# Weight differences of a feed-forward block: GpSimd subtractions replaced by accumulating DMAs, their signs kept in DRAM

## The chip, the core and the metric

The kernel runs on one core of one Trainium2 chip. The metric is the time of one execution in device microseconds; the time before is the median of three runs, 2515.53 us (2514.8 to 2521.83). A core has TensorE (PE, matrix products; PEld is its weight load), VectorE (DVE), ScalarE (ACT), GpSimd (POOL) and SyncE (SP, which here does nothing but issue DMAs), each with a queue of its own that it works through in order, and 16 DMA engines that serve the DMAs of every queue.

## The reference, cut to what matters

Two sequences of 512 tokens, 1024 features, pass three residual blocks: a scan layer with its own gated MLP, a cross product with a quantized context, and a feed-forward block whose weights are made from pairs of matrices:

```python
def _binary_diff_weight(w, base):
    d = w - base
    coeff = jnp.mean(jnp.abs(d))
    return base + coeff * jnp.sign(d)
W1 = _binary_diff_weight(w1, mean_w1)      # each 3584 x 1024 (W2: 1024 x 3584)
W2 = _binary_diff_weight(w2, mean_w2)
W3 = _binary_diff_weight(w3, mean_w3)
h = silu(x @ W1.T) * (x @ W3.T)
return h @ W2.T
```

The mean of |d| runs over the whole matrix, so no weight can be made before all of its pair has been read once. The MLP of the first block has the same form, with plain weights gate_w, up_w and down_w.

## The kernel before, in words

Everything is computed in float32 on tiles of 128 partitions. The stages, by the span of the profiled execution: norms, input projections and scan up to about 370 us; the scan's output product (L564) and the second norm; then a gate loop for the MLP ("m", about 462 to 1150), a down product (to about 1480), and the same two for the feed-forward block ("f": gate loop from about 1497 to 2240, down product to the end).

Each gate loop (`gates`, L646) has 14 rounds of 256 hidden features. A round takes a gate weight, an up weight and a down weight, each 1 MiB, a tile of 128 x 2048. The products go by a seven-product block scheme: `weight_blocks` (L210) forms sums of weight blocks on VectorE, `BlockProduct` (L227) makes 28 matmuls per product into four PSUM banks, and ScalarE copies the first partial product out (`p1`, L249) so that the next additions can use it. `others` (L254) lets TensorE go on with 12 matmuls before one must wait for an addition that reads `p1`. Silu is at L672, the product of gate and up at L677. `down_blocks` (L274) forms the combinations of the down weight, stored to DRAM at L668; the hidden blocks are stored at L680 to L685. The down product (`down`, L691) loads these combinations back into 12 operand tiles, whose order in memory is the argument `places`, behind an empty region of `space` elements per partition.

The differences are needed twice. During the m loop `side` calls `abs_sums` (L824) in each round: for each of the three pairs it loads raw weight and base (1 MiB each, SP), subtracts them on GpSimd (L827) and sums the absolute values on ScalarE (L828, `accum_out`). `find_coeff` (L857) makes the three coefficients during the m down product. During the f loop `ffn_weight` (L975) loads the pair again, subtracts on GpSimd (L984), takes the sign on ScalarE (L985) and forms base + coeff * sign on VectorE (L986) into the weight tile. The first two weights of the f loop are made before it begins (`begun`, L989), between the m down product, the last context products (L905 to L918, with the queries of L887) and the norm that fills `x3T` (L920).

The order of the instructions on each engine is fixed when the program is built, by a scheduler that places them by its own costs; it is not the order of the source. `side` work therefore runs ahead of the rounds it is called in: in SP's queue the 33rd raw weight of `abs_sums` stands ahead of the load of gate 9. Tiles come from pools (`POOLS`, L627) with a fixed number of buffers, and a load waits until the buffer's last reader is done: two weight buffers `w` for gate and up, two `raw` and two `base` for the pairs, one `t8` for the down weight.

Of the kernel before, what the change touches and what calls it, by code (L numbers as in the profile page):

```python
# [10 lines left out]
F32 = mybir.dt.float32  # L11
BF16 = mybir.dt.bfloat16
AF = mybir.ActivationFunctionType
ALU = mybir.AluOpType
# [3 lines left out]
P = 128  # L18
NB = 2
L = 512  # L20
D = 1024
KC = D // P
# [3 lines left out]
GW = 256  # L26
NG = INTER // GW
# [10 lines left out]
def decoder(ctx, tc, a, out):  # L38
    nc = tc.nc
# [3 lines left out]
    acts = ExitStack()  # L43
# [128 lines left out]
    def flat(tl):  # L172
        return tl.rearrange("p a b -> p (a b)")

    def load_w(wp, tag, src, name, shape=(P, KC, GW)):
        wt = wp.tile(list(shape), F32, tag=tag, name=name)
        nc.sync.dma_start(wt, src)
        return wt

    def tiles_waited(**kw):  # L180
        return tc.tile_pool(reuse_waits="tile", **kw)
# [15 lines left out]
    def act_blocks(name, act, tiles):  # L197

        b11, b21 = act[0][:, :4, :], act[0][:, 4:, :]
        b12, b22 = act[1][:, :4, :], act[1][:, 4:, :]  # L200
        t2, t3, t4 = tiles
        for c in range(TPB):
            cs = slice(c * P, c * P + P)
            sub(t3[:, :, cs], b22[:, :, cs], b12[:, :, cs])
            sub(b12[:, :, cs], b12[:, :, cs], b11[:, :, cs])
            sub(t2[:, :, cs], b22[:, :, cs], b12[:, :, cs])
            sub(t4[:, :, cs], b21[:, :, cs], t2[:, :, cs])
        return {1: b11, 2: b21, 3: b22, 4: t4, 5: b12, 6: t2, 7: t3}

    def weight_blocks(pool, name, w):  # L210

        a11, a12 = w[:, :4, :P], w[:, 4:, :P]
        a21, a22 = w[:, :4, P:], w[:, 4:, P:]
        s = pool.tile([P, 3, 4, P], F32, tag="s", name=f"{name}s")
        s2, s3, s4 = (s[:, i, :, :] for i in range(3))
        sub(s3, a11, a21)
        add(a21, a21, a22)
        sub(s2, a21, a11)
        sub(s4, a12, s2)
        return {1: a11, 2: a12, 3: s4, 4: a22, 5: a21, 6: s2, 7: s3}  # L220
# [53 lines left out]
    def down_blocks(t8):  # L274


        b12, b11, b21, b22, t1, t2, t3, t4 = (t8[:, i, :] for i in range(8))
        sub(t3, b22, b12)
        sub(t1, b12, b11)
        sub(t2, b22, t1)  # L280
        sub(t4, b21, t2)

    def hidden_blocks(h):

        a11, a12, a22, a21, s2, s3, s4 = (h[:, i, :] for i in range(7))
        sub(s3, a11, a21)
        add(a21, a21, a22)
        sub(s2, a21, a11)
        sub(s4, a12, s2)
# [4 lines left out]
    with ExitStack() as m:  # L294
# [9 lines left out]
        sp = proj.enter_context(tiles_waited(name="wsum", bufs=2))  # L304
        pl = {
            "p1": proj.enter_context(tiles_waited(name="wp1", bufs=2)),
            "tmp": proj.enter_context(tiles_waited(name="wtmp", bufs=3)),
        }
# [12 lines left out]
        def load_win(g, i):  # L321
            return load_w(wa, "w", a["w_in"][g, i], f"win{g}_{i}")
# [34 lines left out]
        for i, top in enumerate((0, 4, 5)):  # L357
            w = load_win(0, i)
# [191 lines left out]
        h2T = []  # L550
# [73 lines left out]

    POOLS = dict(t8=1, w=2, raw=2, ap=1, sp=2, hp=1, tmp=7, p1=2)  # L627

    def open_pools(g, name, names):

        pl = {x: g.enter_context(tiles_waited(name=f"{name}{x}", bufs=POOLS[x])) for x in names}
        return pl
# [13 lines left out]
    def gates(name, act, acts, g, pl, weights, side, begun):  # L646


        dram = [
            [tc.dram_tile([P, 7, 512], F32, name=f"{name}{x}d{i}") for i in range(NG)] for x in ("h", "w")  # L650
        ]
        with g:
            B = act_blocks(name, act, [pl["ap"].tile([P, 4, L], F32, tag=f"t{i}", name=f"{name}t{i}") for i in (2, 3, 4)])
            for i in range(NG):
                gw, uw, t8 = weights(i)
                if i == 0:
                    gate, up = begun
                    gate.B = up.B = B
                else:
                    gate, up = (  # L660
                        BlockProduct(
                            (odd, 2 + odd, 4 + odd, 6 + odd), pl, f"{name}{x}{i}",
                            weight_blocks(pl["sp"], f"{name}{x}{i}", w), B,
                        )
                        for odd, (x, w) in enumerate((("g", gw), ("u", uw)))
                    )
                down_blocks(t8)
                nc.sync.dma_start(dram[1][i], t8[:, 1:, :])  # L668
                gc = gate.others() if i == 0 else gate.whole()
                sg = [gate.t("s")] + list(gc[1:])  # L670
                for o, c in zip(sg, gc):
                    nc.scalar.activation(o, c, AF.Silu)  # L672
                side(i, pl["raw"])
                uc = up.others() if i == 0 else up.whole()
                h = pl["hp"].tile([P, 7, L], F32, tag="h", name=f"{name}h{i}")
                for slot, s_, u_ in zip((0, 3, 1, 2), sg, uc):
                    nc.vector.tensor_tensor(h[:, slot, :], s_, u_, ALU.mult)  # L677
                last = i == NG - 1
                if last:
                    nc.sync.dma_start(dram[0][i][:, :3, :], h[:, :3, :])  # L680
                hidden_blocks(h)
                if last:
                    nc.sync.dma_start(dram[0][i][:, 3:, :], h[:, 3:, :])
                else:
                    nc.sync.dma_start(dram[0][i], h)  # L685
        acts.close()
        return dram
# [116 lines left out]
    sums = const.tile([P, 3, NG], F32, name="sums")  # L804
    FFN = (("w1", "mean_w1"), ("w3", "mean_w3"), ("w2", "mean_w2"))

    g = ExitStack()
    pl = open_pools(g, "m", ("t8", "w", "raw", "ap", "sp", "hp", "tmp", "p1"))
    cx = g.enter_context(tiles_waited(name="cx", bufs=1))

    def mlp_weights(i):
        gw = load_w(pl["w"], "w", a["gate_w"][i], f"gate{i}")
        uw = load_w(pl["w"], "w", a["up_w"][i], f"up{i}")
        t8 = pl["t8"].tile([P, 8, 512], F32, tag="t8", name=f"down{i}")
        nc.sync.dma_start(t8[:, :4, :], a["down_w"][i])
        return gw, uw, t8

    def ffn_pair(wp, n, i, why):
        return [
            flat(load_w(wp, tag, a[x][i], f"{why}{x}{i}", (P, 4, 512) if n == "w2" else (P, KC, GW)))  # L820
            for tag, x in (("raw", n), ("base", f"mean_{n}"))
        ]

    def abs_sums(i, wp):  # L824
        for j, (n, _) in enumerate(FFN):
            w, base = ffn_pair(wp, n, i, "s")
            nc.gpsimd.tensor_tensor(w, w, base, ALU.subtract)  # L827
            nc.scalar.activation(w, w, AF.Abs, accum_out=sums[:, j, i : i + 1])  # L828
        if i < KC:
            ctx_codes(i // 4, i % 4)  # L830

    loaded = [mlp_weights(0)]
    begun = first_products("m", h2T, pl, *loaded[0][:2])
    dram = gates("m", h2T, acts, g, pl, lambda i: loaded.pop() if loaded else mlp_weights(i), abs_sums, begun)


    acts = ExitStack()
    x3T = [acts.enter_context(tc.tile_pool(name="x3a", bufs=1, side="right", reuse_waits="tile")).tile([P, KC, L], F32, name="x3T0")]
# [16 lines left out]
    coeff = const.tile([P, 3], F32, name="coeff")  # L855
# [114 lines left out]
    x3T.append(acts.enter_context(tiles_waited(name="x3b", bufs=1)).tile([P, KC, L], F32, name="x3T1"))  # L970

    g = ExitStack()
    pl = open_pools(g, "f", ("p1", "sp", "w", "ap", "hp", "raw"))

    def ffn_weight(i, j):  # L975
        n = FFN[j][0]
        w, base = ffn_pair(pl["raw"], n, i, "f")
        if n == "w2":
            to = pl["t8"].tile([P, 8, 512], F32, tag="t8", name=f"fw2{i}")
            dst = to[:, :4, :].rearrange("p a b -> p (a b)")  # L980
        else:
            to = pl["w"].tile([P, KC, GW], F32, tag="w", name=f"f{n}{i}")
            dst = flat(to)
        nc.gpsimd.tensor_tensor(w, w, base, ALU.subtract)  # L984
        nc.scalar.activation(w, w, AF.Sign)  # L985
        nc.vector.scalar_tensor_tensor(dst, w, coeff[:, j : j + 1], base, ALU.mult, ALU.add)  # L986
        return to

    begun = [ffn_weight(0, 0), ffn_weight(0, 1)]  # L989

    def ffn_weights(i):
# [4 lines left out]
    first = first_products("f", x3T, pl, *begun)  # L996
# [2 lines left out]
    for t in range(TPB, NT):  # L999
        contexts[1].normed(t)  # L1000
    q.close()
    pl.update(open_pools(g, "f", ("t8", "tmp")))

    def store(t0, dh):

        j = t0 < TPB
        for cs in [slice(512 * j + Q * dh, 512 * j + Q * dh + Q)] + [slice(512 * (1 - j) + Q * dh, 512 * (1 - j) + Q * dh + Q)]:
            src = pairs[t0 // 2][:, :, cs]
            nc.sync.dma_start(out[t0 * P : (t0 + 2) * P, cs].rearrange("(a p) n -> p a n", p=P), src)

    dram = gates("f", x3T, acts, g, pl, ffn_weights, lambda i, wp: None, first)
    down("f", dram, 10752, (2, 3, 4, 8, 5, 6, 0, 7, 1, 9, 10, 11), store, lambda: None)


# [50 lines left out]
```

## Time and profile before

| what | value |
|---|---|
| median of three runs | 2515.53 us (2514.8 to 2521.83) |
| profiled execution | 2520.54 us, span 2518.6 us, granted TensorE clock 0.990 |
| TensorE busy | 2446.3 us (97% of the span) |
| VectorE, ScalarE, GpSimd busy | 1462.9, 487.3, 487.9 us |
| DMA | 475.39 MB, mean 189 GB/s |
| GpSimd subtractions L827, L984 | 42 each, 198.8 and 209.5 us busy |
| ScalarE L828, L985 | 42 each, 80.3 and 80.2 us busy |
| VectorE L986 | 42, 98.6 us busy |
| loads of raw weight and base, first loop | 42 and 42 of 1024 KB, 8.9 and 10.5 us from issue to landing |
| the same, second loop | 42 and 42 of 1024 KB, 5.0 and 8.4 us |

The span is from the first to the last instruction; the execution's own time is about 2 us more. The page cuts the span into 40 slices and gives each engine's busy share of a slice in tenths, the granted clock, and the mean share of the 16 DMA engines. A wait is put down to what ended last before it ended. TensorE's busy time says when it had work, not that it ran at its peak.

### The profile page before, as it was taken

The page shows a single profiled execution, that of the slowest core. Times are in us where ns is not written, and L with a number is a line of the kernel's source. Part 1 is how long each engine was busy: PE and PEld are TensorE (multiplying, and loading weights), DVE is VectorE, ACT ScalarE, POOL GpSimd, SP SyncE. Part 2 cuts the span into 40 slices and gives each one's busy share as a digit, 9 for nine tenths or more (in the row PEclk, how much of TensorE's full clock was granted, in tenths as well). Part 3 has the DMA queues.
Part 4 walks back from the last instruction along what each step waited for, and adds up shares of the span by engine and source line. Part 5 has one row for each costly group of instructions (what it writes and reads, how often), then busy time and mean ns, then how long its engine had stood idle before and what let it go on. Part 6 is the DMA issues. An engine that isn't in the chain of part 4 may idle for free.

```text
span 2518.6 us, 20181 instructions
## 1 busy us (share of the span) xinstructions
PE 2446.3 (97%) x7492; PEld 1374.1 (55%) x7492; DVE 1462.9 (58%) x1991; ACT 487.3 (19%) x630; POOL 487.9 (19%) x162
## 2 busy tenths in 40 slices
PE   7999999899999999999999987999999999999999
PEld 5445444444444444447888763444444444478888
DVE  4756685546446554434656676666675576455554
ACT  3222243422223222000001224112112112100000
POOL 1002020533424334000000032242332333000000
PEclk9999999899999999999999997999999999999999
DMA  3110033688888888416565232554455464565751
GB/s 135 44 40 34 17 117 109 264 336 337 321 333 351 324 317 329 144 63 212 175 187 163 93 134 96 206 236 192 188 232 199 183 251 190 183 208 166 215 163 63
DMA packets 168578, 475.39 MB, mean 189 GB/s; under 512 B 19745, under 2 KB 124193, under 8 KB 132641
## 3 DMA queue, kind: packets, MB, share of 16 engines
q1 hardware_dynamic: 168480, 474.12, 51.7%
q8 instruction: 59, 0.97, 0.2%
q14 instruction: 39, 0.31, 0.0%
HBM read 362.89 MB, written 111.15 MB: 188 GB/s over the span
## 4 chain that ended last, share of the span: by engine, by line
PE 84%; DVE 6%; DMA 5%; POOL 2%; ACT 1%; issue 1%; SPq 1%; POOLq 0%; DVEq 0%; ACTq 0%
PE op L564 3%; DMA smean_w<-in_mean_w 2%; POOL sw L827 1%; PE dps L348 1%; PE xa L913 1%; DVE fw L986 1%; DMA fmean_w<-in_mean_w 1%; PE y L484 1%; PE cb L476 1%; DMA down<-in_down_w 0%; PE fo1c L724 0%; PE mo4c L724 0%; PE fo3a L724 0%; PE fo6a L724 0%; PE mo1c L724 0%
## 5 line engine op out<-in xcount | busy, mean ns | idle before, releaser
L984 POOL TENSOR_TENSOR fw<-fw,fmean_w 128x2048 f32<-128x2048 f32 x42 | 209.5, 4995 | 442.0 <-DMA fmean_w<-in_mean_w 365.0
L827 POOL TENSOR_TENSOR sw<-sw,smean_w 128x2048 f32<-128x2048 f32 x42 | 198.8, 4735 | 328.5 <-DMA smean_w<-in_mean_w 282.3
L986 DVE SCALAR_TENSOR_TENSOR fw<-fw,coeff,fmean_w 128x2048 f32<-128x2048 f32 x42 | 98.6, 2348 | 87.5 <-ACT fw L985 65.9
L828 ACT ACTIVATE sw<-sw 128x2048 f32<-128x2048 f32 x42 | 80.3, 1911 | 285.9 <-POOL sw L827 285.9
L985 ACT ACTIVATE fw<-fw 128x2048 f32<-128x2048 f32 x42 | 80.2, 1911 | 233.7 <-POOL fw L984 233.7
L510 POOL TENSOR_TENSOR mz<-mz,ys 128x512 f32<-128x512 f32 x16 | 20.7, 1295 | 309.1 <-DVE ys L507 277.0
L195 DVE TENSOR_TENSOR fh<-fh 128x512 f32<-128x512 f32 x42 | 79.0, 1881 | 0.5
L195 DVE TENSOR_TENSOR down<-down 128x512 f32<-128x512 f32 x56 | 55.6, 1005 | 16.0 <-DMA down<-in_down_w 15.4
L564 PE MATMUL op<-wout,mz 128*128 128x512 f32 x128 | 56.6, 592 | 0.0
L91 POOL TENSOR_TENSOR q_r<-q_e,mhalf 128x1 f32<-128x1 f32 x8 | 6.6, 825 | 239.2 <-DVE q_e L87 238.6
L564 PEld LDWEIGHTS op<-wout,mz 128*128 128x128 f32 x128 | 23.9, 190 | 27.7 <-issue 27.5
L195 DVE TENSOR_TENSOR fw<-fw 128x512 f32<-128x512 f32 x56 | 37.5, 689 | 1.3
L913 PE MATMUL xa<-c,c1T 128*128 128x512 bf16 x128 | 30.3, 393 | 5.4 <-DVE hid L916 5.4
L860 POOL MEMSET ones<- 128x128 f32 x1 | 0.2, 206 | 168.3 <-DMA m6b<-mwd 168.3
L118 PE MATMUL h1T<-ident,h 128*128 128x128 f32 x64 | 15.2, 383 | 16.6 <-ACT h L339 10.7
L192 DVE TENSOR_TENSOR hid<-hid,op 128x512 f32<-128x512 f32 x24 | 15.9, 684 | 23.6 <-PE op L564 23.6
L195 DVE TENSOR_TENSOR mh<-mh 128x512 f32<-128x512 f32 x42 | 28.8, 685 | 0.5
L348 PEld LDWEIGHTS dps<-wdt,h1T 128*128 128x128 f32 x128 | 23.7, 272 | 2.4 <-issue 1.8
L913 PEld LDWEIGHTS <-c1T 128*128 128x128 bf16 x128 | 12.9, 101 | 21.6 <-issue 7.2
L583 POOL TENSOR_TENSOR hid<-hid,xa 128x1024 f32<-128x1024 f32 x8 | 20.6, 2577 | 11.3 <-DMA xa<-in_x 9.0
L348 PE MATMUL dps<-wdt,h1T 128*128 128x8 f32 x128 | 22.1, 301 | 0.0
L507 DVE SCALAR_TENSOR_TENSOR ys<-mx,dskip,y 128x128 f32<-128x128 f32 x64 | 18.4, 342 | 5.5 <-PE y L487 4.0
(1975 smaller groups left out, 5344.9 us busy)
## 6 DMA issues: line engine op xcount, KB each, us to landing
sw<-in_w SPq DMA_DIRECT2D x42, 1024.0 KB, 8.9
smean_w<-in_mean_w SPq DMA_DIRECT2D x42, 1024.0 KB, 10.5
fw<-in_w SPq DMA_DIRECT2D x42, 1024.0 KB, 5.0
fmean_w<-in_mean_w SPq DMA_DIRECT2D x42, 1024.0 KB, 8.4
mwd<-down SPq DMA_DIRECT2D x14, 1792.0 KB, 6.8
fwd<-fw SPq DMA_DIRECT2D x14, 1792.0 KB, 6.6
mhd<-mh SPq DMA_DIRECT2D x13, 1792.0 KB, 6.7
fhd<-fh SPq DMA_DIRECT2D x13, 1792.0 KB, 5.7
```

Of the source, the lines that this page charges most:

```text
L195: nc.vector.tensor_tensor(out_, x, y, ALU.subtract)
L348: nc.tensor.matmul(dps[:, t, :], h1T[t // TPB][:, k, c : c + P], wdt[:, k, :], start=(k == 0), stop=(k == KC - 1))
L476: nc.tensor.matmul(cb, o["B"][:, cols], o["C"][:, :, cols], start=True, stop=True)
L484: nc.tensor.matmul(y, o["xt"][:, c, :], att, start=True, stop=(c == 0))
L510: nc.gpsimd.tensor_tensor(o["z"][:, :, cols], o["z"][:, :, cols], ys, ALU.mult)
L564: nc.tensor.matmul(ps, A[p][:, k, t * P : t * P + P], B[p][:, k, :], start=(k == 0), stop=(k == 3))
L827: nc.gpsimd.tensor_tensor(w, w, base, ALU.subtract)
L828: nc.scalar.activation(w, w, AF.Abs, accum_out=sums[:, j, i : i + 1])
L913: nc.tensor.matmul(ps, self.c1T[:, k, c : c + P], self.c2[k // 4][:, k % 4, hs], start=(k == 0), stop=(k == KC - 1))
L984: nc.gpsimd.tensor_tensor(w, w, base, ALU.subtract)
L985: nc.scalar.activation(w, w, AF.Sign)
L986: nc.vector.scalar_tensor_tensor(dst, w, coeff[:, j : j + 1], base, ALU.mult, ALU.add)
```

## The change

In the first loop, a piece of the pair is now handled so: SP loads the base, ScalarE negates it in place, a DMA from GpSimd's queue adds the raw weight to it in SBUF (`accum_op=ALU.add`), ScalarE takes the sign into a 16-bit tile, which SP stores to a DRAM array `signs`, and ScalarE sums the absolute values as before. The three tiles of differences and two of signs come from one pool. In the second loop, SP loads the signs (0.5 MiB instead of two loads of 1 MiB), ScalarE multiplies them by the coefficient straight into the weight tile, and a DMA from GpSimd's queue adds the base there. GpSimd has no subtractions left, VectorE no L986. The weights of even and odd rounds have buffers of their own (`w`, `w1`, two each); the pool order before the second loop, the empty region and the places of the last down product are others.

```diff
-    POOLS = dict(t8=1, w=2, raw=2, ap=1, sp=2, hp=1, tmp=7, p1=2)
+    POOLS = dict(t8=1, w=2, w1=2, raw=1, sign=2, ap=1, sp=2, hp=1, tmp=7, p1=2)
...
-    def ffn_pair(wp, n, i, why):
-        return [
-            flat(load_w(wp, tag, a[x][i], f"{why}{x}{i}", (P, 4, 512) if n == "w2" else (P, KC, GW)))
-            for tag, x in (("raw", n), ("base", f"mean_{n}"))
-        ]
+    signs = [[tc.dram_tile([P, KC * GW], BF16, name=f"sign{j}_{i}") for i in range(NG)] for j in range(3)]
+
+    def piece(n, i):
+        return a[n][i].rearrange("p a b -> p (a b)")
 
     def abs_sums(i, wp):
-        for j, (n, _) in enumerate(FFN):
-            w, base = ffn_pair(wp, n, i, "s")
-            nc.gpsimd.tensor_tensor(w, w, base, ALU.subtract)
-            nc.scalar.activation(w, w, AF.Abs, accum_out=sums[:, j, i : i + 1])
+
+        for j, (n, base) in enumerate(FFN):
+            d = wp.tile([P, KC * GW], F32, tag="raw", bufs=3, name=f"d{n}{i}")
+            nc.sync.dma_start(d, piece(base, i))
+            nc.scalar.activation(d, d, AF.Identity, scale=-1.0)
+            nc.gpsimd.dma_start(d, piece(n, i), accum_op=ALU.add)
+            sg = wp.tile([P, KC * GW], BF16, tag="sign", bufs=2, name=f"sg{n}{i}")
+            nc.scalar.activation(sg, d, AF.Sign)
+            nc.sync.dma_start(signs[j][i], sg)
+            nc.scalar.activation(d, d, AF.Abs, accum_out=sums[:, j, i : i + 1])
         if i < KC:
             ctx_codes(i // 4, i % 4)
...
-    pl = open_pools(g, "f", ("p1", "sp", "w", "ap", "hp", "raw"))
+    pl = open_pools(g, "f", ("p1", "sp", "ap"))
+    g.enter_context(tiles_waited(name="fgap", bufs=1)).tile([P, D], F32, name="fgap")
+    pl.update(open_pools(g, "f", ("sign", "hp", "t8", "w", "w1")))
 
     def ffn_weight(i, j):
-        n = FFN[j][0]
-        w, base = ffn_pair(pl["raw"], n, i, "f")
+
+        n, base = FFN[j]
+        sg = pl["sign"].tile([P, KC * GW], BF16, tag="sign", name=f"fs{n}{i}")
+        nc.sync.dma_start(sg, signs[j][i])
         if n == "w2":
             to = pl["t8"].tile([P, 8, 512], F32, tag="t8", name=f"fw2{i}")
             dst = to[:, :4, :].rearrange("p a b -> p (a b)")
         else:
-            to = pl["w"].tile([P, KC, GW], F32, tag="w", name=f"f{n}{i}")
+            to = pl[("w", "w1")[i % 2]].tile([P, KC, GW], F32, tag="w", name=f"f{n}{i}")
             dst = flat(to)
-        nc.gpsimd.tensor_tensor(w, w, base, ALU.subtract)
-        nc.scalar.activation(w, w, AF.Sign)
-        nc.vector.scalar_tensor_tensor(dst, w, coeff[:, j : j + 1], base, ALU.mult, ALU.add)
+        nc.scalar.activation(dst, sg, AF.Identity, scale=coeff[:, j : j + 1])
+        nc.gpsimd.dma_start(dst, piece(base, i), accum_op=ALU.add)
         return to
...
-    pl.update(open_pools(g, "f", ("t8", "tmp")))
+    pl.update(open_pools(g, "f", ("tmp",)))
...
-    dram = gates("f", x3T, acts, g, pl, ffn_weights, lambda i, wp: None, first)
-    down("f", dram, 10752, (2, 3, 4, 8, 5, 6, 0, 7, 1, 9, 10, 11), store, lambda: None)
+    dram = gates("f", x3T, acts, g, pl, ffn_weights, lambda i: None, first)
+    down("f", dram, 13312, (9, 10, 11, 4, 0, 1, 3, 2, 5, 6, 7, 8), store, lambda: None)
```

In the changed file the lines of the first loop are L827 (base load), L828 (negation), L829 (accumulating DMA), L831 (Sign), L832 (store of the signs) and L833 (sum), those of the second L986 (load of the signs), L993 (scaling) and L994 (accumulating DMA).

More of the change, by code (lines that the diff above doesn't have):

```diff
@@ L672, in gates @@
                     nc.scalar.activation(o, c, AF.Silu)
-                side(i, pl["raw"])
+                side(i)
                 uc = up.others() if i == 0 else up.whole()
@@ L833, in decoder @@
     begun = first_products("m", h2T, pl, *loaded[0][:2])
-    dram = gates("m", h2T, acts, g, pl, lambda i: loaded.pop() if loaded else mlp_weights(i), abs_sums, begun)
+    dram = gates("m", h2T, acts, g, pl, lambda i: loaded.pop() if loaded else mlp_weights(i), lambda i: abs_sums(i, pl["raw"]), begun)
     acts = ExitStack()
```

## The prediction

> **What bounds the kernel now.** I read the page's slices first, then busy time by stretch, then the DMA queue of one stretch, then the order of SP's queue.
>
> The page, part 2:
>
> ```profile
> PE   7999999899999999999999987999999999999999
> ...
> POOL 1002020533424334000000032242332333000000
> ...
> DMA  3110033688888888416565232554455464565751
> ```
>
> TensorE is at 90% or more in nearly every slice, so the kernel is bound by TensorE and an engine beside it is worth only what it makes TensorE wait. The slices at 8 in the DMA row are the first gate loop, the one stretch where a second resource is nearly used up. Busy time by stretch:
>
> ```profile
> core 0: us, PE busy (x) PEld busy (x) DVE busy (x) ACT busy (x) POOL busy (x), PEclk, DMA share, GB/s
> 498.90:880.80 381.90, 381.48 (x889) 168.48 (x889) 206.50 (x253) 94.77 (x113) 135.33 (x30) 1.00 0.85 335
> ...
> 1478.00:1600.00 122.00, 94.94 (x288) 45.78 (x287) 92.64 (x120) 40.89 (x48) 41.41 (x14) 0.86 0.37 146
> 1600.00:2200.00 600.00, 598.18 (x1394) 264.59 (x1393) 374.55 (x404) 113.84 (x112) 172.76 (x35) 1.00 0.53 206
> ```
>
> The first row runs from the load of gate 1 to that of gate 9: TensorE never waits, GpSimd is busy a third of the time and hides completely, but the 16 DMA engines are 85% busy. The second row, the change from the first down product to the second gate loop, is where TensorE idles: 122.0 - 94.9 = 27.1 us, at a clock of 0.86. The third is the second gate loop, with TensorE full and DMA at 0.53. SP's queue by time gives the ends of the first row, eight rounds of 47.7 us:
>
> ```profile
> 498.91 0.33 SPq L177 DMA_DIRECT2D gate<-in_gate_w  x1
> ...
> 880.80 0.33 SPq L177 DMA_DIRECT2D gate<-in_gate_w  x1
> ```
>
> and the DMA view of that stretch what was moved (last column: us to landing):
>
> ```profile
> DMA packets 16055, 127.79 MB, mean 335 GB/s; under 512 B 1744, under 2 KB 1744, under 8 KB 2640
> ...
> sw<-in_w SPq DMA_DIRECT2D x30, 1024.0 KB, 9.2
> smean_w<-in_mean_w SPq DMA_DIRECT2D x30, 1024.0 KB, 10.9
> ```
>
> 127.79 MB took 0.85 of 381.9 us, so the engines move 127.79 / 0.85 = 150 MB in 381.9 us, and one pass of 1 MiB costs 2.66 us of all of them.
>
> **The change, part by part.**
>
> Removed, first loop (L827): 42 GpSimd subtractions of 4.7 us. They lie beside a full TensorE: 0. The raw loads on SP go too, but the same bytes come back as accumulating DMAs from GpSimd's queue.
>
> Added, first loop: per piece a negation and a Sign on ScalarE (1.91 us each, from the 1.91 us of L828, which has the same shape), a store of 0.5 MiB of signs on SP, and an accumulating DMA of 1 MiB. ScalarE goes from 95 to about 95 + 34 x 3.8 = 225 us of the 382: it fits by sum. The DMA engines are the question. In the built program SP's queue holds, after the load of gate 1 up to that of gate 9, 119 MiB (before: 121): 35 base loads, 34 sign stores (17 MiB), 8 gate, 8 up and 13 down loads, 12 + 8 stores of 1.75 MiB, and 3 MiB of context. Nearly the same as before, and the accumulations come on top. The 34 sign stores ahead of gate 9 each wait for a Sign, and that Sign for its accumulation. So TensorE cannot begin round 9 before 119 MiB and 34 accumulations have gone through the engines. Nothing can overtake: both queues' orders are fixed, and ScalarE's copies of p1 (L249), which TensorE needs in each product, stand between Signs in its queue. TensorE has 12 matmuls of 381.5 / 448 = 0.85 us, some 10 us, before it misses such a copy.
>
> The trace of before has no accumulating DMA. Lower end: it moves what a plain load moves, one pass, 2.66 us (not less: the bytes are the same). Upper end: it reads the source, reads the tile and writes the tile, each as dear as a load, three passes, 8.0 us. I take two, 5.3 us: it must read the tile besides the source, and in a plain load the write is already inside the pass. The middle is also nearest to the row of loads, with one stream added.
>
> 119 x 2.66 = 317 us; 34 accumulations take 91, 181 or 272 us with one, two or three passes. Together 408, 498 or 589 us instead of 381.9: +26, **+116** or +207 us. This is at engines never idle; the latencies of the chain (load, negation, accumulation, Sign, store) add to it, and packets that run at the stretch's best pace (slices of 423 to 431 GB/s) take from it. At 427 GB/s one pass would need 160.4 MB / 427 = 376 us, and cost nothing.
>
> The Trainium skill speaks against the change here: Collectives: The Full Stack, section "The bandwidth ceiling: the fold count and why AG ≠ RS ≠ AR", says that an addition inside the DMA engine reads two sources through one ring and so runs at half the pace of a copy (measured ratio 1.93). No run here shows it; by it the accumulations would cost 34 x 2.66 x 1.93 = 175 us, and the loop +110.
>
> After gate 9 three pieces or so are left, beside a DMA share of 0.31 (1000 to 1150 us): 0. Before gate 1 three accumulations stand ahead of it in SP's order; its load has slack, since up 0 is still being multiplied: 0.
>
> Removed, transition: TensorE's waits there are
>
> ```profile
> PE q1T L900 <- ACT qc L161: 9.2, 2, 8.9
> PE xa L913 <- DVE hid L916: 5.4, 1, 5.4
> ```
>
> Both end late because VectorE's small operations last some 4.3 us longer whenever a GpSimd subtraction runs. VectorE by time, while GpSimd is at L984 from 1478.93 to 1489.07:
>
> ```profile
> 1479.17 5.54 DVE L903 SCALAR_TENSOR_TENSOR hid<-hid,q_rs,col 128x1024 f32<-128x1024 f32 x1
> 1484.63 4.46 DVE L902 TENSOR_TENSOR q_rs<-q_rs,s12e_x 128x1 f32<-128x1 f32 x1
> 1489.12 1.28 DVE L903 SCALAR_TENSOR_TENSOR hid<-hid,q_rs,col 128x1024 f32<-128x1024 f32 x1
> ```
>
> The same L903 takes 1.28 us right after, and a second pair of such delays (4.63 and 4.45 us, 1501 to 1512) precedes the other wait. Without subtractions both waits go: 8.9 + 5.4 = **-14 us**. What is late next: the second weight. Its sign load waits for a matmul that ends at 1476; load 3.4 us (the 512 KB rows of c2d), scaling 1.9, accumulation 5 to 11 give 1486 to 1492, against 1497.6 before. So it is not later.
>
> Second gate loop: 42 subtractions and 42 VectorE operations of 2.35 us (L986) go, all beside TensorE: 0. DMA per round falls from 9.4 MiB by 6 and rises by 1.5 + 2 x 3 to 10.9, a share of 0.53 x 10.9 / 9.4 = 0.61: it fits. A weight is made a round ahead (two more buffers, w1): scaling, accumulation and three VectorE blocks need some 15 to 20 us of 47.7. If that cover were gone, some 10 us per round would show.
>
> Last down product: other places, same loads; its first wait was 1.2 us: 0.
>
> Sum against the profiled execution (2520.5 us, span 2518.6): +116 - 14 = 2622. The median of the runs shown is 5 us lower: **2617**.
>
> **Rivals.** (1) Faster: an accumulation is one pass and the packets pack tighter. Then the first loop costs 0 and the transition remains: 2520.5 - 14 - 5 = 2501. It decides as long as 119 MiB and the accumulations fit in 382 us, which at 427 GB/s is up to about one pass. For it: slices over 420 GB/s exist. Against: 335 on average, and a tile that must be read. At the average pace one pass still gives 2527. (2) Three passes, or two with waits between: 2520.5 + 207 - 14 - 5 = 2708. For it: SP holds base loads behind sign stores, so the engines may idle while a chain of load, negation and accumulation runs out. Against: gate, up, down and store traffic fills such gaps. (3) Still dearer: from about 4.3 passes ((47.7 / 2.66 - 5) / 3) the second loop is bound as well and the time is over 2800. Nothing in the profile speaks for it.
>
> **How the numbers follow.** Forecast 0.60 (2575 to 2665 by itself); rival 1 0.16, spread from 2501 up to the 2527 of the average pace, of it 0.12 below 2508 and 0.04 above; rival 2 0.17; rival 3 0.07. A measurement of this kernel tells about 0.3%, 7.5 us, from no change: faster 0.12, same 0.04 (2508 to 2523), slower 0.60 + 0.17 + 0.07 = 0.84. The range takes the bounds of one and three passes, 2510 to 2710; it leaves out 0.12 of rival 1 and rival 3, 0.19.
>
> **What would show it.** Right: gate 9 is loaded some 498 us after gate 1, with a DMA share over 0.9, TensorE waiting for ScalarE's p1 copies or for gate loads, and ScalarE's Sign (L831) waiting for DMA; packets of the accumulations about twice as long as the loads'. VectorE's L902 and L903 are short in the transition. Wrong: 382 us between those loads, or TensorE waiting in the second loop.

## The result and the profile after

The changed kernel takes 2652.13 us (2650.82 to 2659.12) against 2516.16 us (2514.8 to 2521.83) of the kernel before on the same chip: slower, at a ratio of 1.0542 (95%: 1.0517 to 1.0566). The forecast was 2617, the range 2510 to 2710. The profiled execution took 2650.82 us, its span 2649.0 us at a clock of 0.970.

The slices of the page after, in the rows shown of before:

```profile
PE   7999999888777877999999999799999999999999
POOL 1001022100000000000000001000000000000000
...
DMA  3100214999999999512475624566656756455752
```

GpSimd is nearly empty from the first gate loop on (in that loop only the issuing of DMAs is left). In that loop the DMA row has gone from 8 to a run of 9, and above it stand TensorE's 7s and 8s: nearly all of the loss is there. Busy time by stretch (columns as before: us, PE, PEld, DVE, ACT, POOL, clock, DMA share, GB/s):

```profile
512.47:1011.01 498.54, 397.18 (x858) 171.26 (x857) 172.37 (x258) 232.07 (x194) 30.66 (x35) 0.89 0.98 323
1011.01:1079.60 68.59, 55.54 (x123) 24.18 (x122) 20.68 (x32) 30.44 (x27) 3.64 (x5) 0.90 0.95 291
...
1770.00:2250.00 480.00, 479.13 (x1117) 211.60 (x1116) 194.35 (x300) 94.13 (x90) 25.20 (x29) 1.00 0.63 178
```

The first row again runs from the load of gate 1 to that of gate 9: 498.5 us instead of 381.9, the DMA engines busy for 0.98 of it. The second is round 9, still full. The third is the second gate loop: TensorE as full as before, DMA at 0.63. DMA queues of the first stretch (packets, MB, share of the engines' time):

```profile
q1 hardware_dynamic: 17959, 125.26, 62.4%
q0 software_dynamic: 4896, 35.65, 35.4%
```

Queue q0 holds the accumulating DMAs. They took 0.354 x 498.5 / 35.65 = 4.95 us of all engines per MB, the rest 0.624 x 498.5 / 125.26 = 2.48: an accumulation is 2.0 passes. The trace's packet records say the same: 629 ns for 8 KB in the median on q0, 309 ns on q1.

How TensorE meets this, in one place. ScalarE by time, then TensorE by time (start, us; in brackets the idle time before and what ended it):

```profile
736.77 1.91 ACT L831 ACTIVATE sgw<-dw 128x2048 bf16<-128x2048 f32 x1 [11.82 <-DMA dw<-in_w]
738.59 0.57 ACT L249 COPY mg4p<-mg4a 128x512 f32<-128x512 f32 x1
```

```profile
727.13 3.60 PE L238 MATMUL mg4d<-mt,gate 128*128 128x512 f32 x8
739.93 5.43 PE L238 MATMUL mg4b<-mt,mg4s 128*128 128x512 f32 x8 [9.21 <-DVE mg4u L192]
```

ScalarE stood 11.8 us before a Sign whose accumulation had not landed; behind it in the queue stood the copy of p1; VectorE's addition waits for that, and TensorE (`mg4b`) for the addition: 9.2 us. The eight matmuls after the wait took 5.43 us, where the block before it took 3.60.

Where TensorE stands against the kernel before, in us, read from the starts of the same matmuls in the two traces (round 1, round 9, first down product, round 1 of the second loop, last block), for all kernels of this study:

| kernel | m round 1 | m round 9 | m down | f round 1 | end |
|---|---|---|---|---|---|
| changed | +3.5 | +130.2 | +141.1 | +133.2 | +130.8 |
| plain | +1.5 | +52.4 | +54.5 | +47.1 | +43.5 |
| four | +3.6 | +165.2 | +168.6 | +161.0 | +157.7 |
| paced | +0.4 | +73.7 | +77.5 | +92.8 | +90.6 |
| half | +12.4 | +122.9 | +131.2 | +123.2 | +119.8 |
| noact | +2.8 | +136.3 | +141.9 | +137.2 | +141.2 |
| sub_signs | +2.0 | +14.6 | +16.3 | +9.7 | +7.7 |
| sub_noact | +2.2 | +1.5 | -4.7 | -9.9 | -5.4 |
| sub_gsign | +2.3 | +135.8 | +205.6 | +196.8 | +194.0 |
| first_vec | +1.6 | +1.0 | -1.0 | -15.0 | -15.0 |
| sub_vec | +0.1 | +15.0 | +14.6 | -6.5 | -10.4 |
| sep_vec | +0.3 | +13.2 | +13.8 | -7.0 | -10.9 |
| sep_vec2 | 0.0 | -0.7 | -6.8 | -27.5 | -31.4 |

So the first loop cost 141 us, the transition gave 8 back, the second loop and the last down product 2. Each row is read from one execution; eleven runs of sub_signs lie within 8.4 us.

### The profile page after: what moved, and what is told of

Read it like the earlier page. It is cut to its first block, busy times and chain, and to the rows that moved or that the text cites. A ratio compares the mean times of both kernels' runs of the same rounds, so it can differ in the third digit from the quotient of the medians.

```text
span 2649.0 us, 20162 instructions
## 1 busy us (share of the span) xinstructions
PE 2473.4 (93%) x7484; PEld 1381.4 (52%) x7492; DVE 1236.4 (47%) x1949; ACT 642.6 (24%) x714; POOL 152.9 (6%) x162
## 4 chain that ended last, share of the span: by engine, by line
PE 68%; issue 19%; DMA 7%; DVE 3%; POOL 2%; ACT 2%; SPq 0%; POOLq 0%; DVEq 0%; ACTq 0%
PE op L564 3%; DMA dw<-in_w 2%; DMA fw<-in_mean_w 2%; POOL dw L829 1%; DMA dw<-in_mean_w 1%; PE dps L348 1%; PE y L484 1%; PE cb L476 0%; PE fo1c L724 0%; PE mo4c L724 0%; PE fo5a L724 0%; PE mo4a L724 0%; PE mo5a L724 0%; PE mo6a L724 0%; PE mo1a L724 0%
## 5 line engine op out<-in xcount | busy, mean ns | idle before, releaser
L993 ACT ACTIVATE fw<-fsw,coeff 128x2048 f32<-128x2048 bf16 x42 | 83.9, 2000 | 227.0 <-DMA fsw<-sign 27.2
L831 ACT ACTIVATE sgw<-dw 128x2048 bf16<-128x2048 f32 x42 | 80.2, 1909 | 231.5 <-DMA dw<-in_w 221.8
L828 ACT ACTIVATE dw<-dw 128x2048 f32<-128x2048 f32 x42 | 79.8, 1903 | 57.9 <-DMA dw<-in_mean_w 57.7
L195 DVE TENSOR_TENSOR fw<-fw 128x512 f32<-128x512 f32 x56 | 37.7, 690 | 103.9 <-DMA fw<-in_mean_w 103.0
L833 ACT ACTIVATE dw<-dw 128x2048 f32<-128x2048 f32 x42 | 79.9, 1902 | 0.6
L994 POOL DMA_DIRECT2D fw<-in_mean_w x42 | 36.6, 872 | 577.1 <-ACT fw L993 475.4
L829 POOL DMA_DIRECT2D dw<-in_w x42 | 37.1, 883 | 541.8 <-ACT dw L828 541.8
L195 DVE TENSOR_TENSOR down<-down 128x512 f32<-128x512 f32 x56 | 37.6, 690 | 59.6 <-DMA down<-in_down_w 58.8
L564 PEld LDWEIGHTS op<-wout,mz 128*128 128x128 f32 x128 | 23.9, 190 | 27.7 <-issue 27.5
L195 DVE TENSOR_TENSOR mh<-mh 128x512 f32<-128x512 f32 x42 | 28.9, 689 | 0.6
L195 DVE TENSOR_TENSOR fh<-fh 128x512 f32<-128x512 f32 x42 | 28.9, 688 | 0.4
L238 PE MATMUL mg5b<-mt,mg5s 128*128 128x512 f32 x16 | 9.6, 756 | 17.1 <-DVE mg5u L192 17.1
L160 DVE TENSOR_SCALAR ctx<-ctx 128x2048 f32<-128x2048 f32 x8 | 9.8, 1225 | 32.2 <-ACT ctx L159 32.2
L238 PE MATMUL mg9b<-mt,mg9s 128*128 128x512 f32 x16 | 10.2, 798 | 13.1 <-DVE mg9u L192 13.1
L118 PE MATMUL x3T<-ident,f 128*128 128x128 f32 x64 | 10.5, 316 | 12.3 <-ACT f L934 8.3
```

The lines of the kernel that those rows point to most:

```text
L118: nc.tensor.transpose(ps[:, i, :], src[:, k * P : (k + 1) * P], ident)
L195: nc.vector.tensor_tensor(out_, x, y, ALU.subtract)
L564: nc.tensor.matmul(ps, A[p][:, k, t * P : t * P + P], B[p][:, k, :], start=(k == 0), stop=(k == 3))
L828: nc.scalar.activation(d, d, AF.Identity, scale=-1.0)
L829: nc.gpsimd.dma_start(d, piece(n, i), accum_op=ALU.add)
L831: nc.scalar.activation(sg, d, AF.Sign)
```

## The experiments

**The theory** is that of the prediction: in the first loop the DMA engines are full, because an accumulation costs them two passes. **The main rival** says that not the engines but order sets the pace: a piece goes through load, negation, accumulation, Sign and store one after another, with fixed queues, so that SP and ScalarE stand still in front of late steps. Edits are against the changed kernel unless said otherwise. A single time stands for one run.

**plain: the same DMA without the addition.**

```diff
-            nc.gpsimd.dma_start(d, piece(n, i), accum_op=ALU.add)
+            nc.gpsimd.dma_start(d, piece(n, i))
```

> The changed kernel, but the DMA from GpSimd's queue in the first loop copies the raw weight over the negated base instead of adding it to it (so no difference is formed, and signs and coefficients are those of the raw weights). Order of every queue, waits, buffers, bytes named by the DMAs and ScalarE's work stay as in the changed kernel. Theory (the DMA engines are full and an accumulation costs them two passes): 119 MiB + 34 plain MiB = 153 passes of 2.66 us = 408 us between the loads of gate 1 and gate 9 instead of 498, some 15 us less in the rounds around, total 2535 to 2565. Rival (the chain of load, negation, DMA, Sign and store behind each other in fixed queues sets the pace, not the engines): the stretch stays within 20 us of 498 and the total at 2630 or more. Packets of the copies: about 310 ns each by the theory.

2563.54 us; 426 us between the loads of gate 1 and gate 9. The stretch, and its q0:

```profile
507.12:933.18 426.06, 389.27 (x874) 169.21 (x873) 172.71 (x258) 232.10 (x194) 18.86 (x35) 0.96 0.95 378
```

```profile
q0 software_dynamic: 4905, 35.73, 20.6%
```

The same megabytes now cost 0.206 x 426.1 / 35.73 = 2.46 us each, half of 4.95. Nothing but the addition was taken out (SP's queue has the same DMAs in the same order), and the first loop went from +141 to +54.5: the second pass of the 42 accumulations is worth 87 us. The stretch came out 18 us above the 408 forecast: the engines worked 0.95 x 426 = 405 us, as forecast, but 21 us were idle. And even at one pass the change would have lost: in this order more of the pieces' bytes stand ahead of gate 9 than in the kernel before, so that the engines need 405 us where eight rounds take 382.

**four: one more tile of differences** (`bufs=3` to `bufs=4`).

> The changed kernel with four tiles of differences in the first loop instead of three. Theory (engines full): same passes, so 2640 to 2660, gate 1 to gate 9 within 10 us of 498, DMA share 0.97 or more. Rival (the chain of one piece's steps, three pieces at a time, sets the pace): a quarter less time per piece, so the stretch falls toward the 382 us of the kernel before, and the total below 2600.

2677.66 us, slower still; both expectations missed, the rival's by its sign.

```profile
499.39:1041.70 542.31, 412.21 (x889) 177.54 (x888) 173.32 (x261) 240.80 (x200) 30.30 (x35) 0.88 0.94 306
```

The order of SP's queue shifts with the buffer: gate 1 now stands behind one store of signs instead of three and is loaded at 499.4 us instead of 512.5, which is 13 of the 44 us; gate 9 stands behind one base load and one store more and comes 31 us later. Some two more accumulations fall into the stretch, whose engine time is 0.94 x 542 = 510 us (changed kernel: 489), and 33 us are idle. A fourth buffer did not help; why more time is idle was not taken apart.

**paced: a piece may be loaded only when its own round has come.**

```diff
+            nc.scalar.copy(d[:, 0:1], s[j][:, 0:1])     # s: results of Silu of round i
             nc.sync.dma_start(d, piece(base, i))
```

> The changed kernel, but a piece of round i can be loaded only after a Silu result of round i (ScalarE first copies one column of it into the tile), so three pieces per round instead of the four to five that run ahead. Theory (engines full): in SP's order a middle round then holds 13.5 MiB and 3 accumulations of two passes, 19.5 x 2.66 = 52 us against the 47.7 of a round without waits, and the whole first loop some 243 passes = 646 us against about 640; so most of the loss goes, total 2535 to 2590. Rival (the accumulating DMAs and the Signs stand in the way of the rounds wherever they are, whatever the load on the engines): 14 rounds with three pieces each lose as much as 9 rounds with four to five, total 2630 or more.

2609.71 us (ratio 1.0364, 1.0348 to 1.0380): 42 us better than the changed kernel, but above the 2590 that the theory allowed.

```profile
499.34:954.46 455.12, 400.62 (x889) 173.98 (x888) 173.32 (x264) 175.42 (x172) 21.24 (x24) 0.94 0.89 295
```

At 0.89 the engines were not full, and TensorE still lost 73 us up to round 9. So fullness is not all: order costs too, here with the wait for Silu that the edit itself puts ahead of each base load. In the first block of the down product 22 us more were lost (7 came back in the transition), most of them here (TensorE's waits: total, times, longest):

```profile
PE cps L868 <- POOL ones L866: 12.1, 1, 12.1
```

That GpSimd operation sets a tile for the coefficients; by the profile it waited for a store of hidden blocks to land.

**half: only half of every piece is added.**

```diff
+            nc.gpsimd.dma_start(d[:, : KC * GW // 2], piece(n, i)[:, : KC * GW // 2], accum_op=ALU.add)
+            nc.gpsimd.dma_start(d[:, KC * GW // 2 :], piece(n, i)[:, KC * GW // 2 :])
```

> The changed kernel, but only the first half of each raw piece is added in the first loop; the second half is copied over by a second DMA from the same queue (left out: half of every difference, so signs and coefficients are not the reference's). SP's order is that of the changed kernel. Theory (what an accumulation costs goes with its bytes, twice a copy's): half of the way between the 426 us of plain and the 498 us of the changed kernel between the loads of gate 1 and gate 9, 455 to 470, total 2595 to 2615. Rival (each accumulating DMA has a cost of its own, whatever its size, or the wait of the Sign for a DMA sets the pace): 485 or more, total 2635 or more.

2639.56 us, 486 us between the loads: the rival's numbers, not the theory's.

```profile
518.01:1003.69 485.68, 390.98 (x858) 168.66 (x857) 172.40 (x258) 231.74 (x194) 50.15 (x70) 0.91 0.94 332
```

```profile
q0 software_dynamic: 9795, 35.67, 29.1%
```

The engines' own time behaves as the theory says: q0 took 0.291 x 485.7 = 141 us, near the middle (132) of plain's 88 and the changed kernel's 176, and all queues 0.94 x 486 = 457 us against 405 and 489. A cost of each DMA that does not go with its bytes would have left q0 at 176. But elapsed time is not engine time: 29 us were idle (changed kernel: 10), and the forecast had no term for that. Which wait makes them was not taken apart; the run shows what an addition costs the engines, not that the time of the stretch follows it.

**noact: accumulations stay, but ScalarE no longer waits for them.**

```diff
-            nc.scalar.activation(sg, d, AF.Sign)
-            nc.sync.dma_start(signs[j][i], sg)
-            nc.scalar.activation(d, d, AF.Abs, accum_out=sums[:, j, i : i + 1])
+            nc.sync.dma_start(signs[j][i], d[:, : KC * GW // 2])     # the same bytes
```

> The changed kernel without Sign and sum of absolute values on ScalarE in the first loop (left out: signs and sums; the store of 0.5 MiB takes the first half of the difference tile instead, and the second loop reads other 16-bit values of the same size from DRAM, so coefficients and weights are not the reference's). Nothing on ScalarE waits for an accumulating DMA any more, only the stores on SP do; the accumulations stay. Theory (engines full, two passes): SP's order holds 121.4 MiB and some 35 accumulations between gate 1 and gate 9, 191 x 2.66 = 509 us, so the stretch takes 490 to 520 us with a DMA share over 0.95, total 2635 to 2680. Rival (TensorE waits because p1 copies stand behind Signs that wait for their DMA, and with them gone the rounds run through): stretch under 450 us, total below 2600.

2660.91 us, within the theory's numbers.

```profile
507.62:1015.11 507.49, 403.98 (x879) 174.52 (x878) 168.78 (x256) 101.84 (x86) 31.74 (x36) 0.90 0.99 321
```

With the waits on ScalarE gone the loss is the same (+141.9 at the down product), and the engines are busy for 0.99 of the stretch; the scheduler puts two base loads and one store more into it than in the changed kernel. The waits in front of the Signs are thus how TensorE feels the loss in the changed kernel, not what makes it.

**sub_signs: the first loop without accumulations.** Both matrices loaded by SP and subtracted on GpSimd as before; Sign and store stay; second loop as in the changed kernel.

```diff
-            nc.scalar.activation(d, d, AF.Identity, scale=-1.0)
-            nc.gpsimd.dma_start(d, piece(n, i), accum_op=ALU.add)
-            sg = wp.tile([P, KC * GW], BF16, tag="sign", bufs=2, name=f"sg{n}{i}")
+            nc.gpsimd.tensor_tensor(d, d, b, ALU.subtract)       # d, b: raw and base, two buffers each
+            sg = b.bitcast(BF16)[:, : KC * GW]
```

> First loop: raw weight and base are both loaded by SP and subtracted on GpSimd as in the kernel before, no negation and no accumulating DMA, but ScalarE still takes the signs and SP still stores them; second loop as in the changed kernel. Theory (the loss is the accumulations' passes alone): gate 1 to gate 9 holds 119.7 MiB = 318 us of passes, below 382, so no loss in the first loop; the transition keeps its gain of about 8 us; total 2503 to 2515, ratio to the kernel before 0.995 to 1.000. Rival (the Signs on ScalarE ahead of TensorE's p1 copies, or the sign stores in SP's order, make the loss): most of it stays, total 2580 or more. It also shows the second half of the change alone.

2524.57 us (ratio 1.0024, 1.0015 to 1.0032): of the 141 us of the first loop 125 are gone, and the transition gives 7 us. Not all of that is the accumulations: the order also runs less far ahead, with 25 raw loads between gate 1 and gate 9 where the changed kernel has 35 pieces. And 16 us stay, with the engines at 0.83, and the forecast of no loss there was wrong. (The profiled run, 2527.76 us, is near the longest of eleven, 2519.49 to 2527.90; sub_vec and sep_vec repeat the loss with 15 and 14 us.) The stretch, and ScalarE by time:

```profile
502.49:895.42 392.93, 381.49 (x886) 167.38 (x885) 209.71 (x249) 132.72 (x131) 113.25 (x25) 1.00 0.83 322
```

```profile
655.67 1.91 ACT L832 ACTIVATE bw<-dw 128x2048 bf16<-128x2048 f32 x1 [10.70 <-POOL dw L830]
...
659.90 0.56 ACT L249 COPY mu3p<-mu3a 128x512 f32<-128x512 f32 x1
```

A p1 copy behind a Sign and its sum again, now a Sign that waits for GpSimd. Two runs ask whether that makes the 16 us.

**sub_noact** takes Sign and sum out of sub_signs, as noact does.

> sub_signs (GpSimd subtractions in the first loop) without Sign and sum of absolute values on ScalarE (left out: signs and sums; SP stores the first half of the difference tile in place of the signs, same bytes, and the second loop reads other 16-bit values). sub_signs lost 16 us in the first loop with the DMA engines at 0.83. Theory (p1 copies behind a Sign that waits for GpSimd): the loss falls to 4 us or less, total 2506 to 2514. Rival (the stores, which wait for GpSimd ahead of gate and up loads in SP's order, make it): 10 us or more stay, total 2518 or more.

2514.68 us: the first loop goes from +16.3 to -4.7, and TensorE is full from gate 1 to gate 9, without a wait in the profile:

```profile
502.20:882.30 380.10, 380.10 (x887) 168.17 (x886) 199.54 (x249) 37.42 (x52) 115.21 (x25) 1.00 0.87 334
```

Sign and sum on ScalarE made those 16 us; which of the two, the run does not say, but the sum stood there in the kernel before as well. The stores did not make them: they carry the same bytes, as many of them stand ahead of each gate load, and ahead of some up loads one more.

**sub_gsign** takes the sign on GpSimd instead:

```diff
-            nc.scalar.activation(sg, d, AF.Sign)
+            nc.gpsimd.tensor_scalar(sg, d, 0.0, 0.5, ALU.is_ge, ALU.subtract)
```

> GpSimd subtractions and sign stores in the first loop as in sub_signs, but the sign is taken on GpSimd (d >= 0, less 0.5; the coefficient is doubled) instead of ScalarE; SP's order is the same. sub_signs lost 16 us in the first loop. Theory: its p1 copies stood behind Signs that waited up to 19 us for GpSimd, the DMA engines (0.83) having room; with the Sign gone from ScalarE at least half of it goes, total 2506 to 2516. Rival (the sign stores behind GpSimd in SP's order, or the denser GpSimd work that slows VectorE, make the 16 us): 2522 or more.

2715.40 us (ratio 1.0778, 1.0763 to 1.0792), a miss by 200 us, with the DMA engines at 0.65 (560 to 1190 us). GpSimd by time:

```profile
658.60 4.50 POOL L830 TENSOR_TENSOR dw<-dw,bw 128x2048 f32<-128x2048 f32 x1 [13.73 <-DMA bw<-in_mean_w]
663.19 7.40 POOL L832 TENSOR_SCALAR bw<-dw 128x2048 bf16<-128x2048 f32 x1
678.14 4.51 POOL L830 TENSOR_TENSOR dw<-dw,bw 128x2048 f32<-128x2048 f32 x1 [7.55 <-DMA bw<-in_mean_w]
```

The sign takes 7.3 us here against 1.9 on ScalarE. The store waits for it, the next base load stands behind the store in SP's queue, and the next subtraction waits for that load: a piece every 20 us, 60 us per round of three, where a round has 48. This is the rival's chain, with free engines. It is read from the trace; no run took it apart. Two other costs of the edit stand beside it: ScalarE's sum now waits for GpSimd's sign ahead of the p1 copies (442 us of waits from 560 to 1190 us), and VectorE's operations are drawn out (346.2 us for 296, 1.17 us in the mean, against 0.82 in the prediction's first row of before). Their shares stay open.

**first_vec: the kernel before with one edit.**

```diff
-        nc.gpsimd.tensor_tensor(w, w, base, ALU.subtract)
+        (nc.vector if i == 0 else nc.gpsimd).tensor_tensor(w, w, base, ALU.subtract)
```

> The kernel before with one edit: the three subtractions of round 0 of the second loop run on VectorE instead of GpSimd. It does of the change only what the prediction credits: no GpSimd subtraction runs in the transition. Theory (the waits of 8.9 and 5.4 us there are VectorE's operations slowed by GpSimd's subtraction; part of it comes back as waits for the second weight or its norm): the gain of 8 us of the changed kernel or up to 12 comes, total 2505 to 2512, ratio 0.995 to 0.998. Rival (the gain came from the shorter load of signs and the earlier weight, not from the slowed VectorE; two subtractions of 2.35 us more on VectorE delay its own chain): 2515 to 2525.

2504.17 us (ratio 0.9939, 0.9928 to 0.9951). Of the wait of 8.9 us 2.6 are left, that of 5.4 us is gone, and VectorE's small operations are short:

```profile
1482.02 0.15 DVE L902 TENSOR_TENSOR q_rs<-q_rs,s12e_x 128x1 f32<-128x1 f32 x1
1482.20 1.28 DVE L903 SCALAR_TENSOR_TENSOR hid<-hid,q_rs,col 128x1024 f32<-128x1024 f32 x1
```

14 us in the transition (-1.0 to -15.0), what the prediction had credited to the whole change.

**sub_vec** is sub_signs with a second loop without accumulations:

```diff
-        nc.scalar.activation(dst, sg, AF.Identity, scale=coeff[:, j : j + 1])
-        nc.gpsimd.dma_start(dst, piece(base, i), accum_op=ALU.add)
+        nc.sync.dma_start(dst, piece(base, i))
+        nc.vector.scalar_tensor_tensor(dst, sg, coeff[:, j : j + 1], dst, ALU.mult, ALU.add)
```

> sub_signs with another second loop: SP loads the base into the weight tile, and VectorE forms sign * coefficient + base there; no scaling on ScalarE and no accumulating DMA is left anywhere. First loop as sub_signs, 16 us over the kernel before. Theory: the wait of 4.3 us for an accumulation ahead of the second loop goes, since a plain load lands sooner and VectorE needs some 2.4 us, so the transition gains 10 to 14 us against the kernel before instead of 8, and the second loop stays at 0: total 2516 to 2522. Rival (VectorE's 42 operations stand ahead of the additions that TensorE waits for): transition or second loop lose, total 2526 or more.

2509.59 us, below both expectations. The first loop repeats its 15 us, the transition gains 21 us (+14.6 to -6.5) instead of 8, and from there to the end 4 more are gained.

**sep_vec** gives sub_vec's signs tiles of their own, **sep_vec2** also moves the first loop's subtraction to VectorE.

```diff
-            sg = b.bitcast(BF16)[:, : KC * GW]
+            sg = wp.tile([P, KC * GW], BF16, tag="sign", bufs=2, name=f"sg{n}{i}")
-            nc.gpsimd.tensor_tensor(d, d, b, ALU.subtract)
+            nc.vector.tensor_tensor(d, d, b, ALU.subtract)      # sep_vec2 only
```

> sub_vec with one edit: the signs of the first loop get two tiles of their own instead of lying in the tile of the base, so that the next base can be loaded as soon as GpSimd has subtracted, and not only after the Sign and its store. sub_vec lost 15 us in the first loop and gained 22 in the transition. Theory: the subtraction, and with it the Sign that stands ahead of TensorE's p1 copies, is late because the base came late; with tiles of their own half or more of the 15 us goes, total 2495 to 2503, below first_vec's 2504. Rival (the Sign waits as long with a tile of its own, since GpSimd's 4.7 us and SP's order set it): 2506 to 2512 as sub_vec.

> sep_vec with the subtraction of the first loop on VectorE too, so that GpSimd has no work on the weights at all. Theory (what TensorE loses is the time a Sign or an addition stands ahead of a p1 copy): the difference comes 2.4 us sooner (2.3 us on VectorE for 4.7 on GpSimd) and VectorE's operations lose the slowing by GpSimd, but VectorE, in order, now waits for the loads of raw weight and base itself, and TensorE waits for VectorE's additions: within 10 us of sep_vec, more likely slower. Rival (GpSimd's slowness is the whole of the first loop's loss): the first loop comes to within 3 us of the kernel before, total under 2498.

sep_vec: 2510.47 us (ratio 0.9963, 0.9950 to 0.9975), the first loop at +13.8: the theory on the tile fell. sep_vec2: **2489.11 us** (ratio 0.9883, 0.9868 to 0.9898), the best of the study, and again the rival was right. Its stretch from 499 to 881 us, and the operation that replaced GpSimd's:

```profile
499.00:881.00 382.00, 382.00 (x891) 168.94 (x890) 219.16 (x274) 136.53 (x131) 0.00 (x0) 1.00 0.88 335
```

```profile
L830 DVE TENSOR_TENSOR dw<-dw,bw 128x2048 f32<-128x2048 f32 x42 | 96.1, 2288 | 40.0 <-DMA bw<-in_mean_w 40.0
```

TensorE is full at 0.88 of the DMA engines, signs and all. VectorE waited only 40 us in all for its loads, and 2.29 us take the place of 4.68. VectorE's other operations are no longer drawn out by GpSimd either (the sums of L195 on `mh` took 0.69 us in the mean, 0.79 in sep_vec). By themselves these cost nothing in sub_noact, where they took 0.98 us and TensorE had no wait; no run separates the two here.

## Why the prediction was right, and where it was off

- **First loop, gate 1 to gate 9 (+116): right.** The loads stand 498.5 us apart (forecast 498), at a DMA share of 0.98; two passes per accumulation were measured as 2.0, and plain and noact show that it is the added pass on full engines. That the sum came within 1 us is luck: the engines worked 489 us instead of 498, and 10 us of idle time, for which the sum had no term, made up for it. The ratio that the Trainium skill gives for a collective (Collectives: The Full Stack, section "The bandwidth ceiling: the fold count and why AG ≠ RS ≠ AR"), 1.93, made an estimate of +110. The rows of this kernel, which has no collective, say 2.0 and +116.6.
- **"Before gate 1 ...: 0": wrong by 13.6 us.** Gate 1 was loaded at 512.5 instead of 498.9. TensorE began round 1 only 3.5 us late, so the slack was there; but gate 9 came 130.2 us late, which is these 13.6 us and the 116.6 of the stretch. That an earlier gate 1 would have saved them is not shown: in four it was loaded at 499.4 us, and gate 9 came later still.
- **"After gate 9 three pieces or so are left ...: 0": wrong by 11 us.** The row of 0.31 was taken from rounds 11 to 13. Round 9 was still full (0.95 in the second stretch row): 68.6 us to the load of gate 10 instead of 48.1. TensorE lost 17.1 us in it; 6.2 of these came back in round 10, where the kernel before has a stall and this one none.
- **Transition (-14): -8.** The mechanism is right (first_vec: 14 us by taking round 0's subtractions away from GpSimd alone). "Not later" was wrong for what comes after it. The waits there, after:

```profile
PE fg0c L238 <- DVE x3T L195: 6.3, 1, 6.3
...
PE fg0a L238 <- DMA fw<-in_mean_w: 4.3, 1, 4.3
PE x3T L118 <- ACT x3T L121: 3.9, 1, 3.9
```

  The first line is 1.2 us longer than in the kernel before (5.1); the other two are new. The second is an accumulation that TensorE now waits for. In sub_vec, without accumulations, both are gone and the transition gains 21 us.
- **Second loop and last down product (0): right**, -0.6 and -1.8 us; TensorE 479.1 of 480 us, DMA 0.63 for 0.61 forecast.
- **The sum.** 13.6 (start) + 0.6 (the stretch) + 10.9 (round 9) + 6.1 (transition) - 2.4 (end) = 28.8; the rest of the 35 us to 2652 is that the profiled run of before lay 5 us above its median and that of after 1 us below it.
- **Rival 1's price was wrong.** It put one pass at 2501 to 2527; plain took 2564. In this order the 153 passes alone are 405 us of engine time, over the 382 of eight rounds, and there are idle gaps on top. The pace of 427 GB/s that it hoped for was not held: 378.
- **Not in the prediction at all:** that order costs time beside the bytes. The changed kernel hides this, since its engines are full anyway; paced and sub_signs show it, and the idle time of half and the chain of sub_gsign agree with it. How much of paced's loss is ScalarE's queue and how much SP's stays open.

## What to carry to other kernels

Price a DMA that adds (from DRAM into SBUF, float32, as here) as two passes, and add up engine time over the whole run of work that the queues' order puts ahead of the next needed load. Where that passed the time available, the stretches took 1 to 6% longer than the engines worked, and taking work off ScalarE (noact) did not help. An operation that waits for something slow must not stand ahead of a short copy that the busiest engine needs: a Sign of 1.9 us, with its sum behind it, cost nothing by busy time and 16 us by place. Before trading a slow subtraction for DMA traffic, try it on another engine: VectorE did it in half the time, and sep_vec2, which keeps the stored signs but has no accumulating DMA, beat the two kernels by 1.2% and 6%.

## What the runs showed of the hardware that was not expected

- An accumulating DMA from DRAM into SBUF takes 629 ns per packet of 8 KB, a plain one from the same queue 313 ns (plain), loads on SP's queue 309 ns.
- One more buffer made a DMA-bound stretch longer (four: 542 us for 498, 13 of them by an earlier start), with one piece more ahead of its end and 33 us idle instead of 10.
- GpSimd needs 7.3 us to turn a 128 x 2048 tile of f32 into two-valued bf16, ScalarE's Sign 1.91 us.
- TensorE's busy time itself is longer where it waits: 2473.4 us after and 2446.3 us before for the same matmuls (7,484 and 7,492 of them in the traces), at a granted clock of 0.89 in the stretch with waits against 1.00 there before; sep_vec2, which has no wait in the first gate loop, had 2434.9 us.
